# An earlier bound for the merges of a mixture-of-experts tail, and one expert tile's transposes moved ahead of the last first layer

## The chip, the cores and the metric

The kernel runs on one core of a Trainium2 chip. A core has a matrix engine (TensorE, written PE), three further engines for elementwise work (VectorE, written DVE; ScalarE, written ACT; GpSimd, written POOL), a queue engine that here only starts transfers (SyncE, written SP), and 16 DMA engines that move data between the chip's memory and the on-core buffers. The metric is the device time of one execution in microseconds (us); the median of several executions is compared.

## The reference

Two blocks, each with a layer norm in front and a residual sum behind. The first is a linear attention with 32 heads of width 64, the second a mixture of 8 experts of which every token uses its best two:

```python
x = L0_attn_hidden_states                       # (1, 2048, 512), float32
x = x + attn(layernorm(x), Wq, Wk, Wv, Wo, bo)  # q = relu(xWq), k = relu(xWk), v = xWv
                                                # kv = k^T v per head; (q kv) / clip(q . sum k) @ Wo + bo
x = x + ffn(layernorm(x), ...)

def ffn(x, gate_w, gate_b, bias, w1, b1, w2, b2):
    scores = xf @ gate_w.T + gate_b + bias
    top_scores, top_idx = jax.lax.top_k(scores, 2)
    gates = jax.nn.softmax(top_scores, axis=-1)
    comb = jnp.sum(one_hot(top_idx, 8) * gates[..., None], axis=1)
    h = jax.nn.silu(einsum('td,ehd->teh', xf, w1) + b1)     # 512 -> 352
    y = einsum('teh,edh->ted', h, w2) + b2                  # 352 -> 512
    return einsum('ted,te->td', y, comb)
```

## The kernel before, in words

The 2048 tokens are cut into 16 token tiles of 128 (NT = 16). The attention runs first, in stages over four column blocks; it fills the span up to about 810 us. Its last pass also normalizes each token tile for the experts, scores it (`b_s`), ranks its tokens within their experts (`b_r`) and scatters each token's row twice into a memory area `xs_d`, ordered by expert, in blocks of 128 rows.

From there on the unit of work is an **expert tile**: 128 rows of one expert. There are at most 39 (NTT); 37 of them (NE) are always worked on, the last two only if a count says so, in an `If` at L1185 that this input does not enter (37 scatters are in the profile). The first 14 expert tiles (F1) are whole blocks of tokens from the first token tiles; the others come in the order of their block number within the expert, then of the expert. Steps for expert tile i:

- `c_x` (SP) loads its 128 rows `xg` from `xs_d`. From tile 18 on the buffers are two, tag "f1".
- `c_t` transposes them on PE (L249, tile `xgtp`), and ACT and DVE split the result into a high and a low part (L164, `xgT`: ACT writes the high part, DVE subtracts for the low one). DVE then reads the row's gate words (L845).
- `c_h` is the first layer: 12 matmuls and one for the bias into `ph`; ACT applies silu into a slot of `hbuf` (L1033).
- `c_ht` transposes that slot on PE (L1047, `htp`), and ACT and DVE split it into `hT` (L164).
- `c_y` is the second layer: 9 matmuls into `py`.
- `y_out` scales by the gate on ACT (L1129, `ys`, four buffers) and starts a scatter on POOL that adds the 128 rows into the output (L1132). A token's first expert adds to the token's own output row, its second expert to a spare row further down.
- `merge(t)` starts on POOL a transfer that adds the 128 spare rows of token tile t to its output rows (L1140). It may go once every expert tile that can hold one of that token tile's tokens has landed: `last_of[t]` is the bound on that tile's number, and a `hold` on the scatters up to it makes the merge wait for them.

Order. PE, DVE, ACT and SP run in the order in which the program is written (`tc.manual_schedule`). POOL issues the scatters and merges in the order that the listing of instructions shows, one after the other.

Expert tiles 0 to 15 (H1 = 16) first run through the first layer only (loop at L1081); tiles 0 to 12 are written out to memory (`h_out`), because `hbuf` has three slots, and read back later (`h_in`). The second layer's weights come in meanwhile; `prep_w2` (L919) splits one piece of them on ACT (L925) and DVE (L926). Then the second layer of these 16 tiles runs in the order 13, 14, 15, 0, ..., 12 (loop at L1151). From tile 16 on, each turn of the loop at L1164 does the first layer of tile i+1, the transposes of tile i+3 and the second layer of tile i.

Transposes go through the two banks of the tag "aux" (`xgtp` and `htp` share them in turn), so a transpose can begin only when ACT and DVE have read the one before the last. First layers go through the two banks "mm", second layers through the four banks "acc".

Around the change, the end of the loop at L1081 is (tile 15): first layer of 15, transposes of 17, one `prep_w2`, transposes of `htp` for tile 13 (`y_order[0]`), then L1151 begins with `htp` for tile 14 and the second layer of 13. The merge rule before gives `last_of` = 22, 24, 26, 28 for token tiles 0 to 3, 28 for 4 to 10, and 30, 32, 34, 36, 38 for 11 to 15; a merge is due two turns after its bound (LAG), and at most two go per turn.

Of the kernel before, what the change touches and what calls it, by code (L numbers as in the profile page):

```python
# [26 lines left out]
def linear_attention__then__moe_kernel(  # L27
# [41 lines left out]
    E, HF = b1.shape  # L69
    D = 64  # L70
    CC = C // P
    NT = S // P
# [15 lines left out]
    G1 = 11  # L88
    F1 = -(-(2 * G1 * P - E * (P - 1)) // P) // 2 * 2
# [7 lines left out]
    H1 = 16  # L97
# [52 lines left out]
    def mm_bank(name):  # L150
        return ps.tile([P, 512], FP, tag="mm", bufs=2, name=name)

    def aux_bank(name):
        return ps.tile([P, 512], FP, tag="aux", bufs=2, name=name)

    def mm3(o, lhs, rhs, start, stop):
        (lh, ll), (rh, rl) = lhs, rhs
        first = nc.tensor.matmul(o, lh, rh, start=start, stop=False)  # L158
        nc.tensor.matmul(o, lh, rl, start=False, stop=False)  # L159
        nc.tensor.matmul(o, ll, rh, start=False, stop=stop)  # L160
        return first

    def split(hi, lo, src, on=nc.vector):
        return nc.scalar.copy(hi, src), on.tensor_sub(lo, src, hi.bitcast(FP))  # L164
# [262 lines left out]
    def b_t2(t):  # L427
        tp3 = transpose4(xn2s[t], "x2tp")
        x2T = frp.tile([P, CC, P], FP, tag="kk", bufs=2, name="x2T")
        nc.scalar.copy(x2T, tp3)  # L430
        x2Ts[t] = x2T
# [9 lines left out]
    def b_g(t):  # L441

        x2T = x2Ts.pop(t)
        pg = acc_bank("pg")
        for c in range(CC):
            nc.tensor.matmul(pg[:, 0:E], x2T[:, c, :], gw[:, c, :], start=c == 0, stop=c == CC - 1)
        pgs[t] = pg

    def b_s(t):

        pg = pgs.pop(t)
        sc = rc.tile([P, E], FP, tag="sc", bufs=2, name="sc")
        nc.vector.tensor_add(sc, pg[:, 0:E], gsum)
        top = rc.tile([P, 8], FP, tag="top", bufs=2, name="top")
        nc.vector.max(top, sc)
        at = rc.tile([P, 8], U32, tag="at", bufs=2, name="at")
        nc.vector.max_index(at, top, sc)
        ef = rc.tile([P, 2, 1], FP, tag="ef", bufs=3, name="ef")
        nc.vector.tensor_copy(ef[:, :, 0], at[:, 0:2])
        mk = rc.tile([P, 2, E], BF, tag="mk", bufs=3, name="mk")  # L460
        nc.vector.tensor_tensor(
            mk, iota8.to_broadcast([P, 2, E]), ef.to_broadcast([P, 2, E]), ALU.is_equal
        )
        nc.vector.tensor_add(m_all[:, t], mk[:, 0, :], mk[:, 1, :])
        more = xn2s[t][:, C:CX]
        nc.vector.tensor_sub(more[:, 0:1], top[:, 0:1], top[:, 1:2])
        nc.vector.tensor_copy(more[:, 1:2], at[:, 0:1])
        nc.vector.tensor_scalar_add(more[:, 2:3], part, float(S + t * P))
        route[t] = ef, mk

    def b_r(t):

        ef, mk = route.pop(t)
        pr = acc_bank("pr")
        nc.tensor.matmul(pr[:, 0:E], upper, m_all[:, t], start=True, stop=False)
        nc.tensor.matmul(pr[:, 0:E], ones_bf, macc, start=False, stop=True)
        nc.vector.tensor_add(macc, macc, m_all[:, t])
        mr = rc.tile([P, 2, E], FP, tag="mr", bufs=2, name="mr")
        nc.vector.tensor_tensor(
            mr, mk, pr[:, 0:E].rearrange("p (a e) -> p a e", a=1).to_broadcast([P, 2, E]), ALU.mult  # L480
        )
        rk = rc.tile([P, 2, 1], FP, tag="rk", bufs=2, name="rk")
        nc.vector.tensor_reduce(rk, mr, AX.X, ALU.add)
        nc.vector.scalar_tensor_tensor(
            place[:, t, :], ef[:, :, 0], float(SB * P), rk[:, :, 0], ALU.mult, ALU.add
        )
        xn2 = xn2s.pop(t)
        for n in range(2):
            ins = nc.gpsimd.indirect_dma_start(
                xs_d[:, :], at_place(t, n), xn2, None  # L490
            )
            apart(ins, scattered.values())
            apart(ins, loaded.values())
            scattered[t, n] = ins
# [4 lines left out]
    def b_zero():  # L499

        pz = acc_bank("pz")
        nc.tensor.matmul(pz[0:1, 0:E], ones_bf[:, 0:1], macc, start=True, stop=True)
        nc.vector.tensor_add(behind, pz[0:1, 0:E], ends)
# [331 lines left out]
    def c_t(i):  # L835
        tp3 = transpose4(xgs[i], "xgtp")
        if i < HA:
            xgT = region(106 + 4 * (i % 3), 4 * KB).rearrange("p (l c s) -> p l c s", l=2, c=CC)
        else:
            xgT = frp.tile([P, 2, CC, P], FR, tag="kk", bufs=2, name="xgT")  # L840
        split(xgT[:, 0], xgT[:, 1], tp3)
        xgTs[i] = xgT

        more = xgs.pop(i)[:, C:CX].rearrange("p (k a) -> p k a", a=1)
        nc.vector.tensor_reduce(known[:, :, i], more, AX.X, ALU.max)  # L845
# [17 lines left out]
    for s in range(NS - NT):  # L863
        j, t = divmod(s, NT)
# [54 lines left out]
    def prep_w2():  # L919
        e, k = pieces.pop(0)  # L920
        n = P if k < NH - 1 else HL + 1
        hi, lo = w2h[:n, e, k, :], w2l[:n, e, k, :]
        if e < E2:
            nc.vector.tensor_copy(lo.bitcast(FP), hi.bitcast(FP))
        nc.scalar.copy(hi, lo.bitcast(FP))  # L925
        nc.vector.tensor_sub(lo, lo.bitcast(FP), hi.bitcast(FP))  # L926
# [54 lines left out]
    def next_w2():  # L981
        if loads:
            e, k = loads.pop(0)
            load_w2(e, k, w2h if e < E2 else w2l)
# [30 lines left out]
    def c_e(i):  # L1015

        return number(0, i, mybir.EngineType.PE, E - 1)

    def c_h(i):

        e = c_e(i)
        xgT = xgTs.pop(i)
        ph = mm_bank("ph")
        for c in range(CC):
            mm3(
                ph[:, 0:HF], (xgT[:, 0, c, :], xgT[:, 1, c, :]),
                (w1a[0][:, e, c, :], w1a[1][:, e, c, :]), c == 0, False,
            )
        nc.tensor.matmul(
            ph[:, 0:HF], sel2[:, i, :].to_broadcast([P, P]), b1m, start=False, stop=True  # L1030
        )
        hslot[i] = hbuf[:, (i if i < H1 else i + 1) % HB, :]
        nc.scalar.activation(hslot[i][:, 0:HF], ph[:, 0:HF], AF.Silu)  # L1033

    def h_out(i):
        nc.sync.dma_start(hd[i], hslot.pop(i)[:, 0:HF])
# [6 lines left out]
    def c_ht(i):  # L1043
        h = hslot.pop(i)
        tp = aux_bank("htp").rearrange("p (k s) -> p k s", k=4)
        for k in range(NH):
            nc.tensor.transpose(tp[:, k, :], h[:, ts(k, P)], ident)  # L1047
        hT = frp.tile([P, 2, NH, P], FR, tag="hT", bufs=2, name="hT")
        split(hT[:, 0], hT[:, 1], tp[:, 0:NH, :])
        hTs[i] = hT  # L1050
# [16 lines left out]
    y_order = [*range(H1 - HB, H1), *range(H1 - HB)]  # L1067
# [11 lines left out]

    ask = {0: (), 1: (7,), 2: (8,), 3: (9,), 4: (10,)}  # L1080
    for i in range(H1):  # L1081
        c_h(i)
        if i < H1 - HB:
            h_out(i)
        if i == 0:
            b_r(NT - 3)
            b_g(NT - 2)
            b_s(NT - 2)
            b_t2(NT - 1)
        if i == 1:  # L1090
            b_r(NT - 2)
            b_g(NT - 1)
            b_s(NT - 1)
        if i == 2:
            b_r(NT - 1)
        if i >= 2:
            next(steps, None)
        c_t(i + 2)
        if i == 2:
            b_zero()  # L1100
        if 4 <= i < 8:
            b_zeros((2 * i - 8, 2 * i - 7))
        for k in ask.get(i, (i + 6,)):
            if k < H1 + 4:
                c_x(k)
        if i == 2:
            attn.close()
            cw = ctx.enter_context(tc.tile_pool(name="cw", bufs=1, reuse_waits="tile"))
            w2l = cw.tile([P, E, NH, C], FR, name="w2l")
        next_w2()  # L1110

        for _ in range({2: 1, 3: 1, 5: 1, 15: 1}.get(i, 2 if i > 2 else 0)):
            prep_w2()
        if i == H1 - 1:
            c_ht(y_order[0])
            h_in(HB)
    assert not pieces and not loads
    c_gate(0, H1)


    last_of = {
        t: max(min(F1 + 2 * t + E, 2 * (G1 - 1) + E), 2 * t + E) for t in range(NT)
    }
    LAG = 2
    added, merged, gated = {}, {}, {}

# [37 lines left out]
    for i in range(H1, NE):  # L1164
        if i + 1 < NE:
            c_h(i + 1)
            c_gate(i, i + 1)
            c_next(i + 3)
        else:
            c_gate(i, i + 1)  # L1170
        c_y(i)
        if i + 1 < NE:
            c_ht(i + 1)
        y_out(i)
        due = [t for t in range(NT) if t not in merged and last_of[t] + LAG <= i]
        for t in due[:2]:
            merge(t)
            hold([merged[t]], gated[i])

# [63 lines left out]
```

## Time and profile before

| | us |
|---|---|
| median of 3 runs | 1024.8 (1022.13, 1024.8, 1025.36) |
| the profiled execution, its own time | 1025.18 |
| its span, first to last instruction | 1023.4 |
| PE busy in the span | 988.2 |
| mean granted PE clock | 0.989 of full speed |
| merges | 16, on POOL, from 954.2 us |
| adding scatters | 37, on POOL, from 868.5 us |

A row of the timeline gives start, duration, engine, line, operation, output<-input, and in brackets how long that engine was idle before it and what ended the idle time. A row of the windows view gives for one stretch of time each engine's busy time, then the clock that was granted to PE, the share of the 16 DMA engines that was busy (a sum over engines, which can exceed 1 a little) and GB/s. Matmuls overlap; their start times are the better guide. A DMA's row on POOL is the issuing, not the moving; the moving is seen in the DMA view, where queue q0 holds the transfers that POOL starts (scatters, merges) and q1 those that SP starts (`xg`).

### The profile page before, as it was taken

To read this page: it belongs to the slowest core of one execution; us is meant where nothing else is said; L and a number is where in the kernel's file an instruction comes from. 1 tells how busy PE (TensorE), PEld (TensorE's weight loads), DVE (VectorE), ACT (ScalarE), POOL (GpSimd) and SP (SyncE) were. 2 spreads that over 40 slices of the span, in tenths; PEclk is the share of its full clock that TensorE was granted. 3 is DMA by queue.
4 is the path that set the end of the run, shared out by engine and by line. 5 is a ranking of instruction groups with operands and counts; after the bars stand their busy time and mean duration, and the time that the engine had idled before them with its cause. 6 is when DMAs were issued, how large, how long until landed. Compare 5 with 4: busy or idle time off the path is not lost. (4 is left out here: it accounts for less than half of the span.)

```text
span 1023.4 us, 14704 instructions
## 1 busy us (share of the span) xinstructions
PE 988.2 (97%) x4903; PEld 825.8 (81%) x4903; DVE 559.7 (55%) x1382; ACT 345.1 (34%) x677; POOL 190.8 (19%) x225
## 2 busy tenths in 40 slices
PE   8999999999999999999999999999999989999993
PEld 5878877788888888788888888888888877889983
DVE  7873334453344226758656865766787766223330
ACT  4333222332223114324112411223545546444441
POOL 3653120000000010031000000001333210643354
PEclk9999999999999999999999999999999999999997
DMA  6994877865535242344322332348655697976788
GB/s 224 374 349 168 247 271 248 275 230 192 173 124 160 98 130 97 113 134 154 114 93 93 114 103 91 95 160 277 216 190 208 227 318 229 167 113 109 129 150 130
DMA packets 77898, 181.33 MB, mean 177 GB/s; under 512 B 9576, under 2 KB 12936, under 8 KB 77648
## 3 DMA queue, kind: packets, MB, share of 16 engines
q1 hardware_dynamic: 62240, 131.94, 39.2%
q0 software_dynamic: 15584, 48.44, 18.8%
q8 instruction: 43, 0.70, 0.3%
q14 instruction: 31, 0.25, 0.1%
HBM read 108.98 MB, written 79.83 MB: 184 GB/s over the span
## 5 line engine op out<-in xcount | busy, mean ns | idle before, releaser
L284 DVE SCALAR_TENSOR_TENSOR k<-pk,k 128x512 fp32r<-128x512 f32 x64 | 44.0, 687 | 122.1 <-ACT k L283 121.8
L158 PE MATMUL po<-area,qT 128*128 128x512 f32 x256 | 101.6, 397 | 1.5 <-ACT qT L164 1.5
L158 PE MATMUL pq<-area 128*128 128x512 f32 x256 | 102.6, 401 | 0.0
L158 PE MATMUL pk<-area 128*128 128x512 f32 x256 | 101.2, 395 | 0.8 <-ACT area L164 0.7
L160 PE MATMUL pk<-area 128*128 128x512 f32 x256 | 100.0, 391 | 1.0 <-DVE area L164 1.0
L159 PE MATMUL g<-k,xn_hl 128*128 128x512 f32 x256 | 100.8, 394 | 0.1
L160 PE MATMUL pq<-area 128*128 128x512 f32 x256 | 100.6, 393 | 0.0
L160 PE MATMUL g<-k,xn_hl 128*128 128x512 f32 x256 | 100.4, 392 | 0.0
L159 PE MATMUL pk<-area 128*128 128x512 f32 x256 | 99.9, 390 | 0.5 <-POOL area L164 0.3
L159 PE MATMUL pq<-area 128*128 128x512 f32 x256 | 100.3, 392 | 0.0
L159 PE MATMUL po<-area,qT 128*128 128x512 f32 x256 | 99.8, 390 | 0.0
L160 PE MATMUL po<-area,qT 128*128 128x512 f32 x256 | 98.7, 391 | 0.0
L164 ACT CAST qT<-qtp 128x512 fp32r<-128x512 f32 x64 | 36.7, 587 | 176.1 <-PE qtp L249 176.1
L158 PE MATMUL g<-k,xn_hl 128*128 128x512 f32 x256 | 91.0, 394 | 3.6 <-ACT k L283 3.6
L164 ACT CAST area<-raw 128x512 fp32r<-128x512 f32 x86 | 53.1, 621 | 117.4 <-DMA raw<-in_w 62.9
L164 DVE TENSOR_TENSOR area<-raw,area 128x512 fp32r<-128x512 f32 x77 | 53.6, 703 | 65.5 <-ACT area L164 54.7
L1132 POOL DMA_INDIRECT out<-ys,dest x37 | 58.2, 1573 | 119.6 <-ACT ys L1129 107.9
L351 POOL TENSOR_TENSOR x<-x,bo_b 128x512 f32<-128x512 f32 x16 | 21.4, 1348 | 311.9 <-DMA x<-in_x 306.7
L283 ACT ACTIVATE k<-pk 128x512 fp32r<-128x512 f32 x64 | 38.1, 596 | 121.9 <-PE pk L160 121.7
L369 DVE TENSOR_TENSOR qk<-q,ksb 128x512 f32<-128x512 f32 x64 | 44.4, 694 | 32.3 <-ACT q L361 31.6
L412 DVE TENSOR_TENSOR x<-x,po 128x512 f32<-128x512 f32 x48 | 32.9, 686 | 53.0 <-PE po L160 46.6
L361 ACT ACTIVATE q<-pq 128x512 f32<-128x512 f32 x64 | 38.4, 600 | 66.7 <-PE pq L160 42.5
(225 smaller groups left out, 2092.2 us busy)
## 6 DMA issues: line engine op xcount, KB each, us to landing
xn_hl<-xnd SPq DMA_DIRECT2D x48, 512.0 KB
x1d<-x SPq DMA_DIRECT2D x48, 256.0 KB
x<-x1d SPq DMA_DIRECT2D x48, 256.0 KB
w1d<-area SPq DMA_DIRECT2D x44, 256.0 KB
area<-w1d POOLq DMA_DIRECT2D x16, 704.0 KB
xg<-xs_d SPq DMA_DIRECT2D x37, 257.5 KB
xnd<-xn_hl SPq DMA_DIRECT2D x16, 512.0 KB
out<-temp POOLq DMA_DIRECT2D x31, 256.0 KB
```

Source lines behind the costliest of these rows:

```text
L158: first = nc.tensor.matmul(o, lh, rh, start=start, stop=False)
L159: nc.tensor.matmul(o, lh, rl, start=False, stop=False)
L160: nc.tensor.matmul(o, ll, rh, start=False, stop=stop)
L164: return nc.scalar.copy(hi, src), on.tensor_sub(lo, src, hi.bitcast(FP))
L283: relu = nc.scalar.activation(k[:, 0, :], pk, AF.Relu)
L284: nc.vector.scalar_tensor_tensor(k[:, 1, :], pk, 0.0, k[:, 0, :].bitcast(FP), ALU.max, ALU.subtract)
L351: nc.gpsimd.tensor_add(x1s[s], x1s[s], bo_b)
L361: nc.scalar.activation(q, pq, AF.Relu)
L369: nc.vector.tensor_mul(qk, q, ksb[j])
L412: nc.vector.tensor_add(x1, x1, pos.pop(s))
L1132: added[i] = nc.gpsimd.indirect_dma_start(out[:, :], bass.IndirectOffsetOnAxis(dest[:, i : i + 1].bitcast(U32), 0), ys, None, compute_op=A ...
```

## The change

First, `c_ht(13)` and the last `prep_w2` move ahead of `c_h(15)`, out of the place behind `c_t(17)`. Second, the bound becomes `max(F1 + E - 1, 2t + E)`: 21 for token tiles 0 to 6, then 22, 24, 26, 28, 30, 32, 34, 36, 38 for 7 to 15. Third, a merge of the last three token tiles is due one turn after its bound instead of two, and a turn issues two merges if its number is odd and one if it is even.

```diff
     for i in range(H1):
+        if i == H1 - 1:
+            c_ht(y_order[0])
+            prep_w2()
         c_h(i)
@@
-        for _ in range({2: 1, 3: 1, 5: 1, 15: 1}.get(i, 2 if i > 2 else 0)):
+        for _ in range({2: 1, 3: 1, 5: 1, 15: 0}.get(i, 2 if i > 2 else 0)):
             prep_w2()
         if i == H1 - 1:
-            c_ht(y_order[0])
             h_in(HB)
@@
-    last_of = {
-        t: max(min(F1 + 2 * t + E, 2 * (G1 - 1) + E), 2 * t + E) for t in range(NT)
-    }
+    last_of = {t: max(F1 + E - 1, 2 * t + E) for t in range(NT)}
     LAG = 2
@@
         y_out(i)
-        due = [t for t in range(NT) if t not in merged and last_of[t] + LAG <= i]
-        for t in due[:2]:
+        due = [
+            t for t in range(NT)
+            if t not in merged and last_of[t] + (LAG if t < NT - 3 else 1) <= i
+        ]
+        for t in due[: 1 + i % 2]:
             merge(t)
             hold([merged[t]], gated[i])
```

No instruction is added or taken away. The listing of POOL's instructions shows the merges after these scatters (the scatter of expert tile i is called scatter i):

| behind scatter | 23 | 24 | 25 | 26 | 27 | 28 | 29 | 30 | 31 | 32 | 33 | 34 | 35 | 36 |
|---|---|---|---|---|---|---|---|---|---|---|---|---|---|---|
| merges before | 0 | 1 | 0 | 1 | 0 | 1 | 0 | 2 | 2 | 2 | 2 | 2 | 0 | 3 |
| merges after | 2 | 1 | 2 | 1 | 2 | 1 | 1 | 1 | 0 | 1 | 0 | 1 | 1 | 2 |

On PE, the transposes of `htp` for tile 13 stand between `xgtp` of 16 and the first layer of 15. On ACT, the order from the split of `xgT` of tile 16 on is: two pieces of weights, `hT` of 13, the last piece, silu of 15, `xgT` of 17, gates, `hT` of 14 (before: two pieces, silu of 15, `xgT` of 17, the last piece, `hT` of 13, gates, `hT` of 14). DVE follows in the same order. SP's order is the same.

## The prediction

> **What bounds the kernel now.** I read the page's table of engines first, then the chain that ended last, then PE's waits, then the timeline around each place that the change touches.
>
> ```profile
> PE 988.2 (97%) x4903; PEld 825.8 (81%) x4903; DVE 559.7 (55%) x1382; ACT 345.1 (34%) x677; POOL 190.8 (19%) x225
> ```
>
> PE is busy for 988.2 of 1023.4 us, so up to its last matmul (start 1008.19) only a PE stall, a lower PE clock or their removal can count. Behind it lies a tail of 15 us without PE work. The chain of waits holds only that tail (start, length, what):
>
> ```profile
> 1009.60 6.41 DMA out<-ys,dest
> ...
> 1016.65 0.76 POOL out L1140
> 1017.41 0.80 POOLq L1239
> ```
>
> The last scatter (36) is issued at 1009.60 and lands at 1016.01; then the merges of token tiles 14 and 15 go, and the span ends 7.4 us later. So three places can move: the switch from first to second layers (861 to 868 us), the turns in which merges share the DMA engines with `xg` loads, and the landing of scatter 36.
>
> PE's timeline at the switch:
>
> ```profile
> 861.29 0.55 PE L1047 MATMUL htp<-ident,hbuf 128*128 128x128 f32 x3
> 863.17 0.55 PE L1047 MATMUL htp<-ident,hbuf 128*128 128x128 f32 x3 [1.33 <-DVE xgT L164]
> 863.79 0.47 PE L158 MATMUL py<-area,hT 128*128 x1
> ...
> 864.79 0.56 PE L158 MATMUL py<-area,hT 128*128 x1
> ...
> 867.28 0.84 PE L1047 MATMUL htp<-ident,hbuf 128*128 128x128 f32 x3
> 867.78 0.71 PE L158 MATMUL py<-area,hT 128*128 x1
> ```
>
> PE waits 1.33 us for a transpose bank that DVE has not yet read, and from 864.8 on its matmuls come 0.43 us apart instead of 0.23: the first second layer takes 867.78 - 863.79 = 3.99 us, the next ones 2.42. The windows view shows why (PE busy, PE load, DVE, ACT, POOL, granted clock, DMA):
>
> ```profile
> 127.58:130.99 3.41, 1.64 (x8) 1.05 (x6) 2.44 (x8) 1.86 (x8) 0.81 (x2) 1.00 0.60 232
> 161.71:165.13 3.42, 1.53 (x6) 0.96 (x6) 3.18 (x6) 1.90 (x5) 0.00 (x0) 1.00 0.73 239
> 861.45:864.86 3.41, 2.00 (x10) 1.23 (x10) 3.18 (x10) 2.13 (x7) 0.00 (x0) 1.00 0.32 85
> ```
>
> The granted clock falls to 0.50 at 165.1, 830.7 and 864.9 and comes back 3.41 us later each time; all edges lie on one grid of 3.41 us. After the first of these three windows (1.64 us busy, all of it matmuls) it stayed at 1.00, after the second (1.53) it fell. After the third it fell although PE was busy for 2.00 us; 0.93 of that are transposes, so I take matmuls alone to count, 1.07 us there, against a limit between 1.53 and 1.64.
>
> Now POOL's timeline and two turns of the windows view, one without merges and one with four:
>
> ```profile
> 983.60 2.27 POOL L1140 DMA_DIRECT2D out<-out  x2
> ...
> 1007.11 1.60 POOL L1132 DMA_INDIRECT out<-ys,dest  x1 [1.21 <-ACT ys L1129]
> 1009.60 1.57 POOL L1132 DMA_INDIRECT out<-ys,dest  x1 [0.89 <-ACTq L1185]
> 1010.62 1.45 POOL L1140 DMA_DIRECT2D out<-out  x1
> ```
>
> ```profile
> 944.90:949.80 4.90, 4.90 (x30) 4.46 (x30) 1.76 (x7) 2.15 (x5) 1.55 (x1) 1.00 0.59 107
> 987.80:993.30 5.50, 5.10 (x32) 4.41 (x29) 1.77 (x7) 2.54 (x7) 4.04 (x5) 1.00 1.04 186
> ```
>
> A turn without merges takes 4.90 us with the DMA engines 0.59 busy. From 984.5 on, with two merges per turn, they are full until the tail, and the turn from 987.8 takes 5.50. PE's waits name the cause:
>
> ```profile
> PE xgtp L249 <- DMA xg<-xs_d: 0.4, 1, 0.4
> ```
>
> **The change, part by part.** Durations are those of the profiled execution (1025.18 us, span 1023.4, 1.8 around it; 0.4 above the median shown, 1024.8).
>
> *A, the switch.* ACT is late there: silu of tile 14 starts at 859.57, after a wait for the write-out of `hbuf`. Nothing of that moves. From there, in the new order: ACT splits `xgT` of 16 (859.93) and two weight pieces (860.39 to 861.5), then `hT` of 13 (0.5, to 862.0). DVE does the two pieces' low parts (861.21, 1.28 long, to 862.49) and only then `hT` of 13 (0.56, to 863.05). PE: `xgtp` of 16 ends at 858.56; `htp` of 13 needs the bank that DVE frees at 858.84, and ends at 859.4; the first layer of 15 (2.05) at 861.45; `xgtp` of 17 at 862.0; `htp` of 14 needs the bank that holds `htp` of 13, free at 863.05. So the wait of 1.33 becomes 0.3 + 1.05, and the second layer of 13 starts at 863.7 instead of 863.79. What is gained is that `hT` of 13 is whole by then: before, the first four matmuls were spread over 863.79, 864.26, 864.57, 864.79; now six fit at 0.23 us before the clock falls at 864.86, and the seventh comes at 865.1 instead of 866.0: -0.9. The matmuls within the window are then 1.2 us, under 1.53, so by that row the clock still falls. If it stays up, the second layer ends at 865.8 and the next begins at 866.2 (its `hT` is late: gates wait for `xgT` of 17, DVE 864.4, then ACT and DVE split `hT` of 14 to 866.2) instead of 867.78: -1.6. Below, 0, if the two orders wait the same. I take -0.9: the grid's phase is the profiled one. The last piece of weights, done on DVE by 863.7 instead of 863.77, stays covered by the second layer's first matmul.
>
> The Trainium skill ("TensorE: Matmul & The Clock Gate", "What's actually happening") says that the clock goes down after at least one idle window of about 3.4 us, which here would need a longer gap than 1.33 us. The trace's 864.86 shows a fall with 2.00 us busy, so the measurement decides; by the page A would be -1.6 and the sum 0.7 lower.
>
> *B, the stall at 993.* `xg` of tile 36, issued at 985.1, meets the two merges of turn 30 and arrives late: 5.50 - 4.90 = 0.6. Turn 30 now has one merge and turn 31 none. Before, single merges (behind scatters 24, 26, 28) left all turns at 4.90. So -0.6.
>
> *C, new stalls.* Turns 23, 25 and 27 now have two merges, while `xg` loads still run (the last is issued in turn 31). The DMA rows price it: a scatter alone holds q0 from 945.0 to 947.5 (2.5 us), `xg` alone q1 from 947.0 to 949.0; with one merge an `xg` issued at 955.6 ends at 961.8 and is used at 963.2; with two it was issued at 985.1, ended at 992.9 and came 0.6 late. Nearest row: +0.6 for each such turn, 1.8 in all; the other end is 0. Turn 23 starts with empty queues like turn 30, so +0.6 there. In 25 and 27 scatter and merges start late by what is left of the turn before (a merge is 1.5 us of all engines: two moved in 1018.0 to 1021.1), so `xg` is further along when they come: half, +0.3 each. C = +1.2. Above the 1.8 lies the slower rival.
>
> The skill's page on transfers ("DMA: Bandwidth & Descriptors", "Queues, rings and completion order") says that a DMA engine takes turns between its queues packet by packet, which would give `xg` its half at once and no stall. The row of 985.1 to 992.9 shows a load that alone takes 2 us needing more than 5 beside two merges; by the page C would be 0 and the sum 1.2 lower.
>
> *D, the tail.* Before, scatter 36 stood behind a backlog: it took 6.41 us, where scatter 23 (issued 943.30, data until 947.5) took 4.2. Without backlog it would gain 2.2. But merge 13, behind it before (1010.62), now stands ahead of it in the same queue: scatter 35 (1007.11) moves from 1008.9 to 1011.4, merge 13 to 1012.9, scatter 36 to about 1015.0: -1.0. Bounds -2.2 and -0.3 (one whole merge more than I count, 2.2 - 1.5 = 0.7, less 0.4 of receipt). Merge 13 also brings a wait: with the shorter lag it waits for scatter 34 (1002.62). By the two latencies that lands between 1006.8 and 1009.0, and POOL reaches the merge at 1008.1; behind it stand the read of the tile count and scatter 36, which cannot go before 1009.6 anyway. So 0, at most +0.5. The 7.4 us behind the landing stay. Issuing two merges takes POOL 2.27 us; between scatters there are 4.9, so elsewhere POOL hides it.
>
> Sum: -0.9 - 0.6 + 1.2 - 1.0 = -1.3: 1023.9 for the profiled execution, **1023.5** on the median.
>
> **Rivals.**
>
> *Everything opens up:* the clock stays up at the switch (-1.6), no `xg` is late (C = 0), the tail gets its full 2.2: -1.6 - 0.6 - 2.2 = -4.4, 1020.4. For it: the wait at the switch is split in two pieces of which neither is 1.33, the grid's phase need not be the same in each execution, and three single merges cost nothing. Against it: the bank still waits for DVE, and two merges were seen to cost 0.6.
>
> *The DMA engines are full from turn 23 to 30* (the slower side). 8 scatters and loads at 0.59 x 4.9 = 2.9 us and 11 merges at 1.5 are 39.7 us of work in 8 x 4.9 = 39.2. Any loss of rate then makes every `xg` late, not three. It decides once a load takes more than 7.6 us from issue to use (980.2 to 987.8, the normal slack). At 0.6 in each of 8 turns: 4.8 - 0.9 - 0.6 - 1.0 = +2.3; with one stall of the 1.8 us that took the clock down at 165, half of 3.41 more: +4.0, 1028.8. For it: in turn 24 before the change (957.5 to 960.0, merge and load together) the engines were only about 0.75 busy, so the rate is not 1. Against it: a late scatter harms nothing (four `ys` buffers), and `xg` has its own queue.
>
> *The merges just change place:* merge 13 eats the tail's gain (D = 0) and C is its full 1.8: -0.9 - 0.6 + 1.8 = +0.3, 1025.1. For it: the same 16 merges move the same bytes in the same queue.
>
> **How the numbers follow.** Chances: forecast 0.38, everything opens up 0.34, full DMA engines 0.18, change of place 0.10. A measurement of this kernel can tell about 0.3% (3.1 us) from no change, so faster means below 1021.7 and slower above 1027.9. Most of the second case (0.27) and a fifth of the first (0.07) make faster 0.34; slower is most of the third and a little beside it, 0.17; the rest 0.49. The range goes from just under 1020.4 to half of the third case: 1020.0 to 1027.5.
>
> **What would show it.** A: `htp` of 14 starting at about 863 and the first second layer taking under 3.3 us; if the clock never falls, the rival. B and C: PE's waits for `xg` after merges in turns 23, 25, 27, none near 993; turns longer than 4.9 in a row from 24 to 32 would be the slower rival. D: scatter 36 landing 5 to 5.5 us after issue. The forecast is wrong if the switch's wait is gone, or if POOL waits for scatter 34 before merge 13 for over 1 us.

## The result and the profile after

| | before | after |
|---|---|---|
| median of 22 runs each, us | 1025.42 | 1026.55 |
| ratio, 95% interval | | 1.0026 [1.0013, 1.0038] |
| the profiled execution, its own time, us | 1025.18 | 1030.55 |
| its span, us | 1023.4 | 1028.8 |

By the ratio the change made the kernel slower by 2.7 us (1.3 to 3.9); the medians lie 1.1 us apart. A gain of 1.3 was forecast. The measured median lies inside the forecast range, the sign is wrong. Of all executions behind the ratios in this document one, of e13, took 3510 us, and its ratio leaves that one out.

To see where the time went I cut each trace at four PE instructions: *switch*, from the bias matmul of expert tile 14 to that of tile 16; *merge stage*, from the bias matmul of tile 17 to the start of the last second-layer matmul; *tail*, from there to the end of the span. What lies ahead of the bias matmul of tile 14 is untouched by the change and varies by several us from execution to execution (it is 4.2 us longer in this profile of after). The three stages, before to after: switch 47.78 to 46.55 (-1.2), merge stage 99.18 to 101.42 (+2.2), tail 15.21 to 15.19 (0). The switch gave what was hoped for and the merge stage took back more.

PE does the same work as before. Page of after, table of engines:

```profile
PE 989.3 (96%) x4903; PEld 824.7 (80%) x4903; DVE 560.9 (55%) x1382; ACT 345.2 (34%) x677; POOL 190.9 (19%) x225
```

PE's timeline of after at the switch, and two rows of the windows view (busy time of PE, PE load, DVE, ACT, POOL, then granted clock, DMA share, GB/s):

```profile
862.75 0.55 PE L1047 MATMUL htp<-ident,hbuf 128*128 128x128 f32 x3
...
866.84 0.55 PE L1047 MATMUL htp<-ident,hbuf 128*128 128x128 f32 x3 [0.79 <-DVE hT L164]
867.46 0.47 PE L158 MATMUL py<-area,hT 128*128 x1
```

```profile
865.00:868.40 3.40, 2.54 (x14) 1.81 (x14) 3.37 (x11) 2.14 (x6) 0.00 (x0) 1.00 0.31 112
868.40:871.80 3.40, 3.40 (x18) 2.74 (x17) 1.31 (x4) 1.61 (x4) 0.80 (x1) 1.00 0.29 69
```

The wait for the transpose bank is 0.79 us instead of 1.33, and the granted clock stays at 1.00 through the first second layer, where it fell to 0.50 in the profile of before. The first second layer now takes 2.6 us instead of 4.0.

PE's waits between 855 and 1010 us (engine, line, releaser: sum, times, longest), and turns of the merge stage in the windows view of after:

```profile
PE xgtp L249 <- DMA xg<-xs_d: 2.6, 3, 1.1
PE htp L1047 <- DVE hT L164: 0.8, 1, 0.8
```

```profile
956.60:962.70 6.10, 5.10 (x31) 4.42 (x30) 1.92 (x8) 2.70 (x7) 3.67 (x4) 1.00 1.02 188
962.70:967.80 5.10, 5.10 (x29) 4.47 (x30) 1.61 (x6) 1.66 (x3) 2.24 (x4) 1.00 1.00 178
...
977.80:984.00 6.20, 5.07 (x31) 4.37 (x30) 1.92 (x8) 2.70 (x7) 3.92 (x4) 1.00 1.00 182
984.00:989.10 5.10, 5.10 (x29) 4.49 (x30) 1.61 (x6) 1.66 (x3) 1.12 (x2) 1.00 1.02 218
```

Two of the three waits for `xg` lie in the merge stage: 1.00 us at 962.65 and 1.14 at 983.95, the loads that were issued behind the double merges of turns 23 and 27. Each makes its own turn 1.2 to 1.3 us longer than 4.90 and the next one 0.2 longer. The double merge of turn 25 brought no wait, and the old stall at 993 is gone.

The end of POOL's timeline and of the chain of waits, after:

```profile
1012.53 1.60 POOL L1135 DMA_INDIRECT out<-ys,dest  x1 [2.04 <-ACT ys L1132]
1013.54 1.45 POOL L1143 DMA_DIRECT2D out<-out  x1
1015.34 1.63 POOL L1135 DMA_INDIRECT out<-ys,dest  x1 [0.35 <-issue]
1022.14 1.67 POOL L1143 DMA_DIRECT2D out<-out  x2 [5.16 <-DMA out<-ys,dest]
```

```profile
1014.52 0.83 issue
1015.34 6.23 DMA out<-ys,dest
```

The last scatter (36) still takes 6.23 us from issue (6.41 before), although POOL's queue moved nothing from 1008 to 1010: merge 13, issued at 1013.54, stands directly ahead of it.

### The profile page after: what moved, and what is told of

Its sections match the earlier page's. It is cut to its first block, busy times and chain, and to the rows that moved or that the text cites. A ratio compares the mean times of both kernels' runs of the same rounds, so it can differ in the third digit from the quotient of the medians.

```text
span 1028.8 us, 14705 instructions
## 1 busy us (share of the span) xinstructions
PE 989.3 (96%) x4903; PEld 824.7 (80%) x4903; DVE 560.9 (55%) x1382; ACT 345.2 (34%) x677; POOL 190.9 (19%) x225
## 4 chain that ended last, share of the span: by engine, by line
PE 75%; DMA 14%; DVE 4%; ACT 3%; issue 3%; SPq 1%; POOL 0%; POOLq 0%; ACTq 0%; DVEq 0%
PE pq L158 6%; PE pq L160 6%; PE pq L159 6%; PE po L158 5%; PE po L160 5%; PE po L159 5%; PE g L158 4%; PE pk L160 4%; PE g L159 4%; PE g L160 4%; PE pk L158 4%; PE pk L159 4%; DMA out<-ys,dest 4%; DMA raw<-in_w 3%; PE qtp L249 3%
## 6 DMA issues: line engine op xcount, KB each, us to landing
xg<-xs_d SPq DMA_DIRECT2D x37, 257.5 KB, 4.2
```

## The experiments

All stages in us. "Waits" is the sum of PE's waits for `xg` rows in the merge stage and their number; in e2 and e10 the first of the two is listed under a DVE operation, and why it is counted here stands with e10.

| kernel | switch | clock falls at the switch | merge stage | waits | tail |
|---|---|---|---|---|---|
| before, first and second profile | 47.78, 47.56 | yes, no | 99.18, 99.14 | 0.4 (1), 0.4 (1) | 15.21, 15.08 |
| after, first and second profile | 46.55, 45.70 | no, no | 101.42, 103.76 | 2.1 (2), 2.9 (2) | 15.19, 15.37 |
| e1 switch alone | 46.51 | no | 99.45 | 0.7 (1) | 14.71 |
| e2 merges alone | 46.16 | no | 100.25 | 1.1 (2) | 15.42 |
| e3 one merge a turn | 45.26 | no | 99.00 | 0.2 (1) | 16.00 |
| e4 lag of two for all | 46.47 | no | 100.47 | 1.1 (2) | 14.27 |
| e6 no merges in the stage | 47.83 | yes | 98.38 | 0 | 13.60 |
| e7, e13 one a turn, merge 13 last | 46.52, 45.41 | no, no | 99.39, 98.38 | 0.7 (1), 0 | 14.20, 13.92 |
| e8 clumps of four | 46.66 | no | 99.49 | 0.2 (1) | 19.20 |
| e9 as e7, old switch | 48.47 | yes | 98.38 | 0 | 13.77 |
| e10 two scatters left out | 46.07 | no | 100.56 | 1.4 (2) | 14.90 |

### One part of the change at a time (e1, e2)

e1 is after with the merge rule of before; e2 is before with the merge rule of after:

```diff
 # e1, against after
-    last_of = {t: max(F1 + E - 1, 2 * t + E) for t in range(NT)}
+    last_of = {
+        t: max(min(F1 + 2 * t + E, 2 * (G1 - 1) + E), 2 * t + E) for t in range(NT)
+    }
...
-            if t not in merged and last_of[t] + (LAG if t < NT - 3 else 1) <= i
+            if t not in merged and last_of[t] + LAG <= i
...
-        for t in due[: 1 + i % 2]:
+        for t in due[:2]:
```

> The kernel before, with the transposes of tile 13 and the last piece of weights ahead of the first layer of tile 15, and nothing else of the change. Three stage times are read: switch (bias matmul of tile 14 to that of tile 16; 47.8 us before, 46.6 after), merge stage (bias matmul of tile 17 to the last matmul; 99.2 before, 101.4 after) and tail (last matmul to the end of the span; 15.2 in both). Theory: the switch is a gain and the merges are the loss: 46.6, 99.2, 15.2, ratio to before 0.9988. Rival, the switch itself costs or does nothing: 47.8, 99.2, 15.2, ratio 1.000 to 1.0015.

Measured: 1024.9 us beside 1025.73 of before (35 runs), ratio 0.9988 [0.9969, 1.0007].

> The kernel before, with the new bound, the shorter lag and the one-or-two rule, but the switch as before. Theory: 47.8, 101.4 (expert rows late behind two merges, PE waits for them 1 us at a time), 15.2, ratio 1.0022. Rival, the difference between the two kernels is scatter of the stages before 810 us and not the merges: merge stage 99.2 and ratio 1.000.

Measured: 1027.49 us beside the same runs, ratio 1.0014 [0.9997, 1.0032]. In ratio the two halves point in the directions of the table, -1.2 and +1.4 us, though each interval still touches 1. Their sum, +0.2, is below the +2.7 of the whole change; the two intervals, of about 1.9 us to either side, leave room for that, so the ratios give the signs of the halves and not their sizes. The merge stage is 1.1 us longer in e2 than in before, with two waits in place of one, and 1.15 shorter than was expected of it.

### Fewer merges a turn, and a longer lag (e3, e4)

```diff
 # e3, against after
-        for t in due[: 1 + i % 2]:
+        for t in due[:1]:
 # e4, against after
-            if t not in merged and last_of[t] + (LAG if t < NT - 3 else 1) <= i
+            if t not in merged and last_of[t] + LAG <= i
```

> The changed kernel, with one merge per turn at most, behind each scatter from 23 to 35. Theory, a turn with two merges is what makes the expert rows late: no PE wait for rows, merge stage 98.6, switch 46.6, tail 15.2 (a merge still stands ahead of scatter 36), ratio 0.998. Rival, the DMA engines are simply full from turn 23 to 30 (2.9 us for scatter and load and 1.5 for a merge in 4.9 leave 10%, less any loss of rate): waits in many turns, merge stage 101 or more, ratio 1.001 or above.

Measured: 1025.63 us, ratio 0.9992 [0.9972, 1.0012]; merge stage 99.00. With at most one merge a turn one wait of 0.23 us is left. The tail is the longest but one, 16.00: a merge goes behind scatter 34 and another behind 35, ahead of scatter 36, which lands 6.65 us after its issue.

> The changed kernel, with the lag of two turns for the last three token tiles too, so that merge 13 is issued behind scatter 36 as before, while no backlog is left there. Theory, merge 13 ahead of scatter 36 eats what the shorter backlog gives: scatter 36 lands 4.7 to 5.2 us after issue instead of 6.2, tail 13.9, the rest like the changed kernel, 1.2 us below it, ratio to before 1.001. Rival, the landing of the last scatter takes 6.2 us with or without a merge ahead: tail 15.2, ratio 1.0026 as for the change.

Measured: 1027.57 us, ratio 1.0016 [0.9998, 1.0035]. Nothing but the place of the late merges differs from after, and the tail falls from 15.19 to 14.27. Merge 13 now goes behind scatter 36, which lands 4.89 us after its issue. The chain of waits of e4:

```profile
1011.87 1.45 issue
1013.52 4.89 DMA out<-ys,dest
```

So the shorter lag of the last three token tiles is what ate the tail's gain. The merge stage keeps its two waits (0.57 and 0.56), so the ratio stays above 1.

### What the merges cost altogether (e6)

```diff
 # against after
-            merge(t)
-            hold([merged[t]], gated[i])
+            merged[t] = None
```

> Changed kernel with the merges of turns 23 to 35 left out: only the merges of token tiles 14 and 15, behind scatter 36, remain, so token tiles 0 to 13 lack the addition of the second expert's rows. It shows what the merges cost altogether. Theory (every wait for xg rows between tile 23 and 31 comes from a merge on the same DMA engines, and the tail's 6.2 us of scatter 36 come from merge 13 standing ahead of it): no wait of PE for xg behind turn 22, all turns 4.9 to 5.0 us, merge stage (bias matmul of tile 17 to the last matmul) about 98.6 us against 101.4 in the profile of the changed kernel; scatter 36 lands 4.2 to 4.9 us after its issue, so the tail (last matmul to end of span) is 13.3 to 14.0 us against 15.2. Rival (the loads are late for another reason, scatters and loads alone being too much for the engines): waits for xg in turns 23 to 27 remain and the stage stays above 100 us. Rival for the tail (a scatter takes 6 us whenever it is the last one): tail stays at 15 us.

Measured (one execution, 1025.85 us, with the lower clock at the switch): no wait for `xg` in the merge stage, all turns 4.9, stage 98.38, tail 13.60. So the waits come with the merges. The end of POOL's timeline in e6:

```profile
1009.41 1.56 POOL L1135 DMA_INDIRECT out<-ys,dest  x1 [2.93 <-DVE dest L859]
1012.08 1.57 POOL L1135 DMA_INDIRECT out<-ys,dest  x1 [1.11 <-ACTq L1191]
1017.32 1.72 POOL L1143 DMA_DIRECT2D out<-out  x2 [3.67 <-DMA out<-ys,dest]
```

The last merges start 5.2 us after the issue of scatter 36 although nothing else is in the queue. The row of 4.2 us by which I had priced an unhindered scatter counted to the end of its data; what follows it comes about 1 us later.

### One merge a turn and merge 13 behind scatter 36 (e7, e13, e9)

```diff
 # e7 and e13, against after
-            if t not in merged and last_of[t] + (LAG if t < NT - 3 else 1) <= i
+            if t not in merged and last_of[t] + LAG <= i
...
-        for t in due[: 1 + i % 2]:
+        for t in due[: 2 if i == 32 else 1]:
 # e9: the same, and c_ht(y_order[0]) and the last prep_w2() back in their places of before
```

> Changed kernel with a merge schedule drawn from the runs so far: lag of two for all tiles, one merge behind each of scatters 23 to 31, two behind 32 (no xg load is left then), one behind 33 and 34, none behind 35, and merge 13 behind scatter 36. Theory (two merges in a turn make the xg load late by 1.0 to 1.4 us, one merge costs 0.1 to 0.2, and merge 13 ahead of scatter 36 costs 0.9): switch 45.3 to 46.5 us, merge stage 98.9 to 99.3 us, tail 14.1 to 14.6 us; ratio to the kernel before 0.997 to 0.999. Rival (the engines are full whatever the pattern, and only the number of merges counts): merge stage 100.5 us or more, ratio 1.001 or above.

Measured: 1021.99 us beside 1023.77 of before (23 runs), ratio 0.9985 [0.9968, 1.0001]. One load was late even so (0.65 us, issued 963.62, 8.30 us to landing), which makes the stage 99.39.

> The merge schedule of the kernel with one merge a turn and none ahead of scatter 36, with the order of transposes at the switch as in the kernel before. A second look at the switch: over the stretch from the bias matmul of tile 14 to the transposes of the third second layer, the old order took 9.45 us in one profile (the clock fell) and 8.08 in another (it stayed up), the new one 7.4 to 8.5 in four. Theory (the reordering itself saves 0.1 us, what differed was whether the clock fell): 8.0 to 8.2 if the granted clock stays 1.00 there, about 9.4 if it falls; the ratio is within 0.001 of that of the kernel with the new order. Rival (the new order keeps the clock up, as a gain of its own): the clock falls here again and the ratio is 0.0010 to 0.0015 higher than with the new order.

Measured: 1024.15 us, ratio 0.9988 [0.9964, 1.0012]. No wait for `xg` at all with the very merges of e7, so a single merge is near the edge, not safely inside it. At the switch the clock fell again, and the stretch took 9.78 us, so what separates the profiles most is whether the clock falls, though 9.78 is above the 9.4 that was expected for a fall; the ratio difference of 0.0003 to e7 is far inside both intervals and tells nothing. The stretch of PE's windows in e9 and in e13 at that place:

```profile
861.01:864.42 3.41, 2.01 (x12) 1.30 (x11) 3.34 (x10) 2.13 (x6) 0.00 (x0) 1.00 0.28 95
...
862.80:866.20 3.40, 3.14 (x10) 2.29 (x11) 2.28 (x9) 0.84 (x3) 0.00 (x0) 0.74 0.34 100
```

```profile
862.80:866.20 3.40, 3.33 (x16) 2.49 (x17) 2.15 (x8) 1.07 (x4) 0.00 (x0) 1.00 0.19 53
```

In e9 the clock falls at 864.42, behind a window with 2.01 us of PE work, 1.19 of it transposes. In e13 it stays up.

> The schedule with one merge a turn and merge 13 behind scatter 36, a second measurement, since the first left its ratio at 0.9985 with 1 inside reach. Theory: 0.997 to 0.999. Rival (a waiting load somewhere in the nine single turns gives back what the tail gains): 0.9995 or above.

Measured: 1021.53 us (median of 12) beside 1023.32 of before (17 runs), ratio 0.9983 [0.9962, 1.0004]. No wait in the merge stage. Twice a gain of about the same size, 1.5 and 1.7 us by the ratio, twice with an interval that just reaches 1: this version is better than the changed kernel (1.0026 against before), and against before it is likely but not proven better.

### Is it the number of merges? (e8)

```diff
 # against e7
-        for t in due[: 2 if i == 32 else 1]:
+        for t in due[: 4 if i % 4 == 3 else 0]:
```

> Same kernel as the last, with the same merges clumped: four behind scatter 23, four behind 27, three behind 31, the others behind 34 to 36; none in the turns between. On average as many merges per turn as in the changed kernel up to turn 30 (11 against 12). Theory (what makes a load late is the number of merges issued between its issue and its use): one wait of PE for xg rows behind scatter 23 and one behind 27, of 2.5 to 5 us each, and nothing between; merge stage 104 to 108 us. Rival (the engines are full on average, and a clump only moves the waits): the sum of waits is that of the changed kernel, merge stage 101 to 102 us. Second rival (the load has its own share of the engines and a clump costs no more than two merges): one wait of about 1.2 us for each clump, merge stage 100.5 to 101.5.

Measured (one execution, 1028.46 us): my theory fell. Four merges behind scatter 23 made PE wait for 0.18 us, four behind 27 for too little to be listed; the stage is 99.49, below every range I had set. POOL's and PE's timeline in e8:

```profile
948.35 3.92 POOL L1143 DMA_DIRECT2D out<-out  x4
952.58 1.62 POOL L1135 DMA_INDIRECT out<-ys,dest  x1 [0.31 <-issue]
```

```profile
957.88 0.63 PE L249 MATMUL xgtp<-ident,xg 128*128 128x128 f32 x4 [0.18 <-DMA xg<-xs_d]
```

The load behind the clump was issued at 949.86 and landed 7.88 us later. Beside two merges it took 8.65 in after and 8.22 in e4. So in this execution the load got a share of the engines of its own, and merges beyond the second cost it nothing more. (The tail of 19.20 comes from two merges ahead of scatter 36 and was not what the run was for.)

### Is it the scatter behind the merges? (e10)

The DMA view in steps of 1 us shows the share of the engines that q1, the load's queue, had behind scatter 23:

| us after the load's issue | 3 to 4 | 4 to 5 | 5 to 6 | 6 to 7 | 7 to 8 |
|---|---|---|---|---|---|
| after (issued 953.86): q1 share, % | 35 | 20 | 21 | 10 | 6 |
| e8 (issued 949.86) | 33 | 26 | 15 | 6 | 1 |

Most of it moves at once and a last part drags. In after the next scatter's data begin while it drags, in e8 they queue behind the four merges. That gave a second theory, tested by leaving those scatters out:

```diff
 # against after, in y_out
+        if i in (24, 28):
+            return
         added[i] = nc.gpsimd.indirect_dma_start(
```

> Changed kernel with the scatters of tiles 24 and 28 left out, those that follow the double merges of turns 23 and 27 (the two waits in the profile of the changed kernel); the rows of these two tiles are missing from the output. All 16 merges stay. Theory (a load beside two merges still gets 20 to 35% of the DMA engines; it is late because its last quarter comes when the next scatter begins, which leaves it 6 to 10% until that scatter is done): the load issued behind scatter 23 lands 6 to 7 us after issue instead of 8.65, no wait of PE for xg behind turns 23 and 27, merge stage 98.4 to 99.8 us against 101.4. Rival (the two merges alone make the load late): waits of about 1 us stay at both places, merge stage 100.5 or more.

Measured (one execution, 1024.31 us): the waits stayed. PE's and POOL's timeline in e10:

```profile
957.47 0.63 PE L249 MATMUL xgtp<-ident,xg 128*128 128x128 f32 x4 [0.88 <-DVE gates L860]
978.02 0.63 PE L249 MATMUL xgtp<-ident,xg 128*128 128x128 f32 x4 [0.51 <-DMA xg<-xs_d]
```

```profile
951.13 0.78 POOL L1145 DMA_DIRECT2D out<-out  x1 [1.51 <-ACT ys L1132]
```

Both waits are there without the scatters, and the stage is 100.56. (The first is put down to a DVE operation of 0.15 us that ended 0.1 before; in the turn before, that operation comes after the transposes, so it isn't what they need. I take the load, issued at 948.8, to be what came last.) So no scatter is needed for a late load. But the edit did not leave the load alone with the two merges: without scatter 24 POOL issued the merge of turn 24 early, at 951.13, 2.3 us after the load, where in after scatter 24 comes 2.4 us after it, and behind the other pair it was the same (971.98, 2.3 us after the load). Whether two merges with nothing behind them make a load late is therefore not shown, and the theory falls only as far as it named the scatter. Which of the 16 engines holds the load's last packets, and why four merges hold them no longer than two, the trace does not show either. That stays open.

### How far it repeats (e11, e12)

Both kernels unaltered, a second profile each.

> The changed kernel unaltered, a second profile, to see how far its waits repeat. Theory (the wait depends on how the load falls against the next scatter, so it varies from execution to execution, but a double merge brings one often): one to three waits for xg rows behind double turns, merge stage 100.0 to 101.5, tail 15.0 to 15.5. Rival (the waits belong to the schedule and are fixed): 1.0 and 1.1 us at the same two places, merge stage 101.4.

Measured (1033.19 us): waits of 1.21 us at 963.03 and 1.65 at 984.67, at the same two places, merge stage 103.76. The places are fixed, as the rival had it, the lengths are not, and the stage is longer than either allowed. The second wait had a consequence. Rows of e11's timeline and windows:

```profile
984.67 0.63 PE L249 MATMUL xgtp<-ident,xg 128*128 128x128 f32 x4 [1.65 <-DMA xg<-xs_d]
```

```profile
982.57:985.98 3.41, 1.69 (x10) 1.13 (x10) 0.15 (x1) 1.14 (x3) 2.33 (x2) 1.00 1.07 228
...
984.90:988.30 3.40, 3.33 (x12) 2.54 (x11) 0.76 (x2) 0.59 (x1) 0.00 (x0) 0.66 1.06 185
```

It left a window of 3.41 us with 1.69 us of PE work, and the clock fell at 985.98 for the next 3.4 us: half of that, 1.7 us, on top of the wait.

> The kernel before, a second profile. Theory (a stall at its first run of double turns at the end, and a clock at the switch that falls in some executions and stays in others): merge stage 98.4 to 99.5, tail 14.7 to 15.4; stretch from the bias matmul of tile 14 to the transposes of the third second layer 8.0 to 8.2 or 9.4 to 9.5, nothing between. Rival (the fall belongs to the old order): 9.4 to 9.5.

Measured (1026.47 us): merge stage 99.14, tail 15.08, one wait of 0.4, as in the first profile. At the switch the wait of 1.33 us is there, and the clock did not fall; the stretch took 8.75 us, between the two values I had allowed:

```profile
863.35 0.55 PE L1047 MATMUL htp<-ident,hbuf 128*128 128x128 f32 x3
865.22 0.55 PE L1047 MATMUL htp<-ident,hbuf 128*128 128x128 f32 x3 [1.33 <-DVE xgT L164]
865.85 0.47 PE L158 MATMUL py<-area,hT 128*128 x1
```

So the old order does not always lose the clock: it fell in 2 of 4 profiles with the old order, in 1 of 10 with the new.

## Why the prediction was wrong, step by step

**A, the switch: -0.9 forecast, about -1.2 found; the way there was another, so the size is in part luck.** Over the profiles the switch takes 47.5 us on average in the old order (4) and 46.3 in the new (10), -1.2, with a spread of about 1 within each; e1's ratio says -1.2 as well, with an interval that reaches 0. The wait became 0.7 to 1.1 us, as the step said (1.05). But the step had the clock fall all the same and took the gain from six matmuls done before. In nine of ten profiles the clock did not fall at all, which the prediction had as the bound of -1.6; in the two profiles compared, that is what happened. Part of the gain seems to need no clock: without a fall, the stretch from the bias matmul of tile 14 to the transposes of the third second layer takes 7.9 us on average in the new order (9 profiles, 7.3 to 8.8) and 8.4 in the old (2, 8.1 and 8.75); with a fall it takes 9.3 to 9.8 (3). The rest may be a smaller chance of a fall: the emptiest window of the clock's grid (3.41 us from edge to edge) at this place holds 2.15 to 2.77 us of PE work in the new order and 1.98 to 2.46 in the old, and the three falls came behind 2.00, 2.01 and 2.15. One fall in ten profiles against two in four is too few to prove that. That it depends on the grid's phase stood in the rivals; e12 and e6 show it from both sides.

What the step took the clock to count does not hold. It let matmuls alone count, against a limit between 1.53 and 1.64 us. Two successive windows of e2, on that run's grid:

```profile
864.80:868.21 3.41, 1.98 (x13) 1.27 (x11) 3.41 (x9) 2.47 (x6) 0.00 (x0) 1.00 0.35 115
868.21:871.62 3.41, 3.41 (x17) 2.87 (x17) 1.23 (x7) 1.64 (x4) 0.27 (x1) 1.00 0.19 53
```

The first holds 1.47 us of transposes, so by the prediction's subtraction 0.51 of matmuls, and yet the clock stayed at 1.00 behind it.

The rule of the Trainium skill that was weighed there ("TensorE: Matmul & The Clock Gate", "What's actually happening": down after an idle window of about 3.4 us) gave -1.6, with a clock that stays up as it did in the profile of after. And yet, if idle means without PE work, the runs speak against it: the clock fell behind 3.41 us with 2.15 us of PE work in e6 and 1.69 in e11, in neither of which PE was idle for more than 1.65.

**B, the stall at 993: -0.6 forecast, about -0.9 found.** It is gone in after. Its price before is 0.8 (99.18 and 99.14 against 98.38 without any wait, e6) to 1.1 (e1).

**C, new stalls: +1.2 forecast, +3.0 in the first profile, +1.9 in e2, +5.4 in e11. This is the step that failed most.** It priced "+0.6 for each such turn", the stall of before, with half of it in turns 25 and 27. The mechanism, a load that is late beside two merges, was right, the size wrong, in three ways. A load beside a fresh pair of merges took 8.65 us in after and 8.86 in e11 (8.22 in e4) against the slack of 7.6 between issue and use, a wait of 1.0 to 1.2 (0.6 in e4) and not 0.4. A wait costs more than its length: the bias matmul, which runs just ahead, and the transposes behind it take 0.36 us longer in all, and with "wait + 0.36 for each" the stage comes out for before, e1, e2, e3, e7 and e10 within 0.1 us, and for after and e4 within 0.3 (e8 is 0.6 longer than its one listed wait explains). And turn 27 did not find the queues half done: turn 25 had no wait, turn 27 a full one. In e11 the clock came on top. The other rule weighed ("DMA: Bandwidth & Descriptors", "Queues, rings and completion order": an engine takes turns between its queues packet by packet, from which the prediction worked out no stall) is met by e8, where further merges cost the load nothing, but not by the 8.65 us of a load whose data alone take 2.

**D, the tail: -1.0 forecast, 0 in the profiles compared (+0.3 on average, 15.33 against 15.0), outside the step's own bounds of -2.2 and -0.3. This step failed too: the gain was not there.** "Without backlog it would gain 2.2" set the end of a scatter's data (4.2 us after issue; the row of 943.30 is scatter 22's, not 23's) against a landing: an unhindered scatter 36 lands 4.89 us after issue (e4), so the gain open was 6.41 - 4.89 = 1.5. Merge 13 ahead of it then took 6.23 - 4.89 = 1.3, and scatter 36 was issued 1.73 us after the start of the last matmul instead of 1.41, 0.3 later (1.59 in e4, where merge 13 is not ahead). 1.5 - 1.3 - 0.3 is nothing left. The wait of merge 13 for scatter 34 cost nothing visible, as forecast.

Together: -1.2 for the switch, +2.5 for the merge stage (99.26 on average in three profiles with the old rule, 101.8 in three with the new), +0.3 for the tail, +1.6; measured +2.7 (1.3 to 3.9). The difference of 1.1 lies within that interval and is not accounted for.

**The rivals.** *The merges just change place* named the tail rightly (merge 13 eats the gain, D = 0) but gave the merge stage too little, like the forecast. *The DMA engines are full from turn 23 to 30* had the size (+2.3 to +4.0) and, with "one stall that takes the clock down", what e11 shows; but its mechanism, a stall in each of eight turns, is not there: two turns stall and the others take 4.9 to 5.2. *Everything opens up* was right for the clock in most profiles and wrong for the loads and the tail.

## What to carry to other kernels

Price a transfer's delay against its slack (issue to use) and not against a stall that happened to be small: the load here lives with 7.6 us, needed about 8 to 9 behind two of the three pairs of transfers on another queue and mostly less than 7.6 behind a single one. Spreading the same transfers evenly lengthened the merge stage by 0 to 1.0 us (e3, e7, e9, e13, against 98.38), pairing them by 1.9 to 5.4 (after, e2, e4, e11); why clumps of four cost only 1.1 (e8) is open. Merge 13 ahead of the last transfer in its queue cost 0.9 us at the end (e4); leave the queue empty for that transfer, and put work that need not land early behind it. When two profiles differ at a place where a clock or another state on a grid can fall either way, take a second profile of the old kernel before crediting the edit.

## What the runs showed of the hardware

- A PE stall at the transposes costs its length and 0.36 us more (in e7 one wait of 0.65 us makes the stage 99.39 instead of 98.38); the excess was the same within 0.1 us in six kernels, and about 0.45 for each wait in after.
- Four 256 KB merges issued in a row delayed a 257.5 KB load on another queue no more than two do (7.88 us to landing in e8 against 8.65, 8.86 and 8.22 in after, e11 and e4).
- The clock fell behind windows of 3.41 us in which PE was busy for 2.00 (before), 2.01 (e9), 2.15 (e6) and 1.69 us (e11), and stayed up behind one with 1.98 (e2). Without the transposes the falls come behind 1.07, 0.82, 0.95 and 1.06 us and the stay behind 0.51. Neither sum separates the falls from the stays; what the clock counts is open.
